# Layer 2's blocks without layer 3's steps among the scores, more steps per network tile, tokens turned one tile earlier, and pins behind the gelus

## The chip, the cores and the metric

The kernel runs on one core of a Trainium2 chip. Five engines work side by side, each through its own queue in order: TensorE (PE; its weight loads are shown apart as PEld), VectorE (DVE), ScalarE (ACT), GpSimd (POOL) and SyncE (SP), which here issues most DMAs. The metric is the device time of one execution in microseconds. The median of 8 runs before the change is 2606.69 us (2600.69 to 2609.49).

## What is computed

A tower of four layers over 8 sequences of 256 tokens with 512 channels, all in float32. Each layer adds a gated attention to the context and then a gated network. The part that matters is layer 2 and the attention of layer 3:

```python
def _L2_xattn_ref(q, k, v):
    scaled = jnp.einsum('bsd,bse->bde', q, k) * scale
    attn = jax.nn.softmax(scaled, axis=1)
    return jnp.einsum('bde,bse->bsd', attn, v)
...
def _L2_ffn_ref(x, proj1, proj1_bias, proj2, proj2_bias, gate_w):
    h = jax.nn.gelu(jnp.einsum('lne,he->lnh', x, proj1) + proj1_bias, approximate=False)
    return jnp.einsum('lnh,eh->lne', h, proj2) + proj2_bias
...
            def step(carry, kv_t):
                aa, bb, pp = carry
                ww = u + kt
                q = jnp.maximum(pp, ww)
                y_t = (exp(pp - q) * aa + exp(ww - q) * vt) / (exp(pp - q) * bb + exp(ww - q))
                q2 = jnp.maximum(pp + w, kt)
                new_carry = (exp(pp + w - q2) * aa + exp(kt - q2) * vt, exp(pp + w - q2) * bb + exp(kt - q2), q2)
...
    x = x + jnp.tanh(g_xattn[2]) * _L2_xattn_ref(_layernorm(x, axis=-1), ctx_2048, ctx_2048)
    x = x + jnp.tanh(g_ffn[2]) * _L2_ffn_ref(_layernorm(x, axis=-1), ...)
    x = x + jnp.tanh(g_xattn[3]) * _L3_xattn_ref(8, 256, 512, td, tf, _layernorm(x, axis=-1), ctx_2048)
    x = x + jnp.tanh(g_ffn[3]) * _L3_ffn_ref(_layernorm(x, axis=-1), ...)
```

Layer 2's attention is channel by channel (a 512x512 matrix for each sequence). Layer 3's attention is a recurrence along the tokens; its network is a mixture of 8 experts with 2 shared ones, for which each token's two experts are chosen ("routing").

## The kernel before

The tokens are 16 tiles of 128 (`xt[t]`), in 4 blocks of 4 tiles (512 tokens, two sequences). `back()` computes layers 2 and 3. Its order is: attention of block 0 and 1 (`xattn2`), network of block 0 (`ffn2`), attention 2, network 1, attention 3, network 2, network 3, then layer 3's shared experts (`shared3`) and routed experts.

`xattn2` makes, for each of its two sequences (`bb`), four score tiles `s`. For each, VectorE takes the maximum (L1562, L1563), ScalarE the exponential `E` with its sum (L1564), and VectorE divides the context by the sum (L1567, L1568, tile `kxvs`). Then four products `o`, two for each sequence, are added to `xt` by VectorE (L227, `add_scaled`).

`ffn2` goes through the 2048 hidden units in four groups `q` of 512. Four tiles `h2p` of hidden units (gelu on ScalarE, L1628) are followed by four output tiles `o2f` (added by L227). One weight load `p` of 512 KB on SyncE belongs to each hidden tile; 7 are held.

Between these, other work is spread in small steps. A generator in `rest` is advanced by `step(n, behind)`, n steps at a time, wherever a score, a hidden tile or an output tile has been issued; its first VectorE instruction of each step (`held`) is ordered behind the instruction given as `behind`. For the network of block 0 the generator is `later_results`: it loads and adds the last sums of layer 1's experts (`combine`: three loads `more` on SyncE and three additions L1529 for each token tile) and loads two blocks of context. Afterwards it is `tail(blk)`: layer 3's attention for a block whose layer 2 is done (`xattn3`), followed by its routing (`route`). `xattn3` normalises and turns the tokens, then for each of four groups of 128 channels runs scans `pp`, the terms `q` and `ex`, one exponential of 2048 elements a partition (L1685), the scans `aa` and `bb`, and the quotient (`num`, `den`, a reciprocal of 3.35 us, L1711). At the end the result is turned back (L1723). At the first output tile of a network's last group `last` runs what is left of the generator (`step(1000)`). In `shared3` the steps go on with the tail of block 3, until 18 pieces of it are issued; then the table of the choices is completed and read back (`slots`, `who_ps`), which the routed experts wait for.

`ready2` is a second generator, for the network of the block before: it normalises that block's tokens among the second sequence's scores (four advances) and turns them (`tr_f`, two tiles at an advance) among the products (two advances).

Instructions are put into their queues at build time, by a scheduler that goes by the order of the program and by when their inputs are ready. `behind(one, other, ...)` sets an order for that scheduler alone and adds no semaphore. The exponential and the gelu need different tables on ScalarE, so a change from one to the other is preceded by a table load.

Of the kernel before, what the change touches and what calls it, by code (L numbers as in the profile page):

```python
# [14 lines left out]
AF = mybir.ActivationFunctionType  # L15
# [7 lines left out]
KC = C // P  # L23
# [26 lines left out]
def flamingo_kernel(ctx: ExitStack, tc: tile.TileContext, a):  # L50
    nc = tc.nc
# [82 lines left out]
    def behind(one, other, reason):  # L134

        tc.add_manual_dep(
            one.ins,
            other.ins.name,
            mybir.DependencyInfo(mybir.DependencyClass.NoSync, mybir.DependencyReason.SCHED_ONLY),
            reason=reason,  # L140
        )
# [71 lines left out]
    def matmul_k(ps, lhsT, rhs):  # L213
        n = len(lhsT)
        for k in range(n):
            one = nc.tensor.matmul(ps, lhsT[k], rhs[k], start=(k == 0), stop=(k == n - 1))  # L216
            if k == 0:
                first = one
        latest[:] = [one]
        return first  # L220

    def mmtile(name):
        return mm.tile([P, BLK], F32, tag="mm", name=name)

    def add_scaled(i, ps, scale):

        return nc.vector.scalar_tensor_tensor(xt[i], ps, scale, xt[i], ALU.mult, ALU.add)  # L227
# [1285 lines left out]
                pass  # L1513


    def combine(tiles, after=(), adds=None, pool=None):

        for t in tiles:
            for u in range(SUMS1):
                if pool is not None and u < 2:  # L1520
                    if u == 0:
                        both = pool.tile([P, 2, C], F32, tag="b8", name=f"more{t}")
                    more = both[:, u, :]
                else:
                    more = t2.tile([P, C], F32, tag="t2", name=f"more{t}_{u}")
                one = nc.sync.dma_start(more, results[u][ts(t, P), :])
                for other in after:
                    behind(one, other, "not before it in the queue")
                add = nc.vector.tensor_tensor(xt[t], xt[t], more, ALU.add)  # L1529
                if adds:  # L1530
                    behind(add, adds[0], "its place")
                    adds[:] = [add]
        return one
# [3 lines left out]
    def load_kx(b, b8, after=None):  # L1537
        t = b8.tile([P, 4 * C], F32, tag="b8", name=f"kxvs{b}")
        kx = t[:, 0 : 2 * C].rearrange("p (t e) -> p t e", t=2)
        one = nc.sync.dma_start(kx, a["ctx"][ts(b, S), :].rearrange("(t p) e -> p t e", p=P))  # L1540
        if after is not None:
            behind(one, after, "not before it in the queue")
        kx_load[:] = [one]
        return kx, t[:, 2 * C :].rearrange("p (k s) -> p k s", k=KC)

    def xattn2(blk, xns, pools, step, ready=iter(())):


        scale = 1.0 / float(np.sqrt(C))
        parts = []  # L1550
        for bb in range(BLK // S):
            b = blk * (BLK // S) + bb
            kx, vs = kxvs.pop(b) if b in kxvs else load_kx(b, pools[0])
            E = pools[bb].tile([P, KC, C], F32, tag="b8", name=f"E{b}")
            parts.append((vs, E))
            z = sm.tile([P, KC], F32, tag="z2", name=f"z2_{b}")
            m = sm.tile([P, KC], F32, tag="m2", name=f"m2_{b}")
            for ec in range(KC):
                ps = mmtile(f"s2_{b}_{ec}")
                matmul_k(ps, [kx[:, t, ts(ec, P)] for t in range(2)], [xns[bb * 2 + t] for t in range(2)])  # L1560
                c1 = slice(ec, ec + 1)
                nc.vector.tensor_reduce(m[:, c1], ps, AX.X, ALU.max)  # L1562
                nc.vector.tensor_scalar(m[:, c1], m[:, c1], -scale, None, ALU.mult)  # L1563
                nc.scalar.activation(  # L1564
                    E[:, ec, :], ps, AF.Exp, bias=m[:, c1], scale=scale, accum_out=z[:, c1]
                )
                nc.vector.reciprocal(z[:, c1], z[:, c1])  # L1567
                one = nc.vector.tensor_scalar(  # L1568
                    vs[:, ec, :], ctxT[blk][:, ec, ts(bb, S)], z[:, c1], None, ALU.mult
                )  # L1570
                if bb:
                    latest_dve[:] = [one]
                    next(ready, None)
                else:
                    step(1, one)
        for bb, (vs, E) in enumerate(parts):
            b = blk * (BLK // S) + bb
            for nt in range(2):
                ps = mmtile(f"o2_{b}_{nt}")
                other = latest[0]  # L1580
                one = matmul_k(
                    ps, [vs[:, ec, ts(nt, P)] for ec in range(KC)], [E[:, ec, :] for ec in range(KC)]
                )
                if bb == 0 and nt == 0:
                    behind(one, other, "the last scores first")
                if bb:
                    next(ready, None)
                one = add_scaled(blk * TB + bb * 2 + nt, ps, tg[:, 2:3])
                step(1, one)


    turned2, latest_dve = {}, []

    def ready2(blk, b8, gb2):

# [16 lines left out]
    def ffn2(blk, b8, wp, b1, gb2, step, last, write):  # L1612
        xT = turned2.pop(blk)

        for q in range(HID // BLK):
            h = b8.tile([P, KC, BLK], F32, tag="b8", name=f"h2_{q}_{blk}")
            p2 = []
            for j in range(KC):
                c = q * KC + j
                w = wp.tile([P, 2 * C], F32, tag="w", name=f"p12_{blk}_{c}")  # L1620
                one = nc.sync.dma_start(w, a["p12"][c])
                if blk == 0:
                    behind(one, first_loads[0], "not before it in the queue")
                p1 = w[:, 0:C].rearrange("p (k o) -> p k o", k=KC)
                p2.append(w[:, C:])
                ps = mmtile(f"h2p_{q}_{blk}_{j}")
                matmul_k(ps, [p1[:, k, :] for k in range(KC)], [xT[:, k, :] for k in range(KC)])
                one = nc.scalar.activation(h[:, j, :], ps, AF.Gelu, bias=b1[:, c : c + 1])  # L1628
                if q == 0:
                    t = blk * TB + j  # L1630
                    nc.gpsimd.tensor_tensor(out=xt[t], in0=xt[t], in1=gb2, op=ALU.add)
                step(2 if q < 1 else 3, one)
                write(1, latest[0])
            for i in range(TB):
                ps = mmtile(f"o2f_{q}_{blk}_{i}")
                matmul_k(ps, [h[:, j, ts(i, P)] for j in range(KC)], p2)
                one = add_scaled(blk * TB + i, ps, tg[:, 6:7])
                step(1, one)
                if q == HID // BLK - 1:
                    last(i)  # L1640

# [9 lines left out]
    def xattn3(blk, b8, lp, u, w, held):  # L1651
# [4 lines left out]
        for c in range(KC):  # L1656
# [7 lines left out]
            bb = lp.tile([P, NS, S + 1], F32, tag="bb", name=f"bb{nm}")  # L1664
# [11 lines left out]
            ex = b8.tile([P, 4, NS, S], F32, tag="b8", name=f"ex{nm}")  # L1676
            q = t2.tile([P, NS, S], F32, tag="t2", name=f"q3_{nm}")
# [4 lines left out]
            held(nc.vector.scalar_tensor_tensor(ex[:, 2], p0, wc, p1, ALU.add, ALU.subtract))  # L1682
            yield
            nc.gpsimd.tensor_tensor(out=ex[:, 3], in0=k, in1=p1, op=ALU.subtract)
            nc.scalar.activation(ex, ex, AF.Exp)  # L1685
            yield
            ev = t2.tile([P, NS, S], F32, tag="t2", name=f"ev3_{nm}")
            nc.gpsimd.tensor_tensor(out=ev, in0=ex[:, 3], in1=v, op=ALU.mult)
# [30 lines left out]
        other = latest[0]  # L1719
        for i in range(TB):  # L1720
            ps = tr.tile([P, KC, P], F32, tag="tr", name=f"y3_{blk}_{i}")
            for c in (KC - 1, *range(KC - 1)):
                one = nc.tensor.transpose(ps[:, c, :], xnT[:, c, ts(i, P)], ident)  # L1723
# [8 lines left out]
    def back():  # L1732
        with ExitStack() as st:
# [110 lines left out]
            place = []  # L1844
# [8 lines left out]
                        reason="spread over the other block's products",  # L1853
                    )

            rest = []

            def step(n, behind=None):

                for _ in range(n):  # L1860
                    if rest:
                        place[:] = [behind] if behind is not None else []
                        if next(rest[0], True):
                            rest.pop()
# [19 lines left out]
            for bb in range(BLK // S):  # L1884
                tiles = (2 * bb, 2 * bb + 1)
                loaded = combine(tiles, kx_load) if bb else first_loads.pop()
                kxvs[bb] = load_kx(bb, bp, loaded)
                xns += norm_of(tiles, f"a2{bb}_")
                other = latest_norm[0]
# [6 lines left out]
            loaded = combine(range(TB, 2 * TB))  # L1896
# [50 lines left out]
            def later_results():  # L1947

                for t in range(2 * TB, TT):
                    loaded = combine((t,))  # L1950
                    yield
                for blk in range(2, NB):
                    context(blk, loaded)
# [164 lines left out]
            one, other = nc.tensor.matmul(cnt, onesb, run[:, TT, :], start=True, stop=True), latest[0]  # L2118
# [93 lines left out]
            other = latest[0]  # L2212
            for n in range(2):
                one = nc.tensor.transpose(who_ps[:, n, :], slots[:, :, n], ident)
# [229 lines left out]
```

## Time and profile before

| | |
|---|---|
| median of 8 runs | 2606.69 us |
| profiled execution, its own time | 2604.53 us |
| its span, first to last instruction | 2602.6 us |
| mean granted TensorE clock | 0.980 |
| busy in the span: PE, DVE, POOL, ACT | 2451.3, 1277.4, 902.2, 643.6 us |

The stages that the change touches, from the busy time in stretches of the span (us; the clock is the granted TensorE clock):

| stretch | what | PE busy | DVE busy | ACT busy | clock |
|---|---|---|---|---|---|
| 1474 to 1509 | attention 1 | 30.37 of 35 | 34.10 | 7.40 | 0.96 |
| 1620 to 1663 | attention 2 | 36.00 of 43 | 33.18 | 10.47 | 0.92 |
| 1662 to 1780 | network 1 | 116.16 of 118 | 81.15 | 28.86 | 1.00 |
| 1780 to 1822 | attention 3 | 34.32 of 42 | 34.23 | 10.48 | 0.96 |
| 1821 to 1943 | network 2 | 118.17 of 122 | 82.11 | 29.73 | 1.00 |
| 1943 to 2066 | network 3 | 118.33 of 123 | 88.28 | 35.28 | 1.00 |
| 2066 to 2235 | first shared experts | 164.52 of 169 | 97.97 | 36.28 | 0.98 |

In the lines of the profile, a name such as `o<-E,kxvs` says what is written from what, `x24` how many records are merged, and a float32 product of 512 columns is two records for each 128 rows. In a timeline the first number is the start and the second the length; the bracket holds the engine's idle time before the line and what ended it. In the view of the waits the numbers are the total, the count and the longest.

### The profile page before, as it was taken

How to read it: one execution, taken by the hardware profiler on the slowest of the kernel's cores; microseconds unless marked ns; L12 is line 12 of the kernel's file. 1: busy time of each engine (PE TensorE's matmuls, PEld its weight loads, DVE VectorE, ACT ScalarE, POOL GpSimd, SP SyncE). 2: the span in 40 equal slices, each digit the busy share in tenths (PEclk: the TensorE clock that was granted, in tenths of full speed). 3: DMA queues.
4: the chain of work that ended last, by engine and by line, in shares of the span. 5: the costliest groups of instructions: out<-in, count | busy, mean ns of one | idle time of the engine just before them, and what ended most of it. 6: DMA issues, size and time to landing. Idle time of an engine off the chain costs nothing. (4 is left out here: it accounts for less than half of the span.)

```text
span 2602.6 us, 29842 instructions
## 1 busy us (share of the span) xinstructions
PE 2451.3 (94%) x10389; PEld 1260.1 (48%) x10404; DVE 1277.4 (49%) x3518; ACT 643.6 (25%) x1451; POOL 902.2 (35%) x843
## 2 busy tenths in 40 slices
PE   7889898999999989999999999898999999999997
PEld 3444454446655635555554344444444444455553
DVE  6656665635656542222222932668676676111111
ACT  1544444411111112222222211222223222111110
POOL 1110201121455355566664010332424252444442
PEclk9999999989999999999999999999999999999999
DMA  5000010011312248899996822021121212898984
GB/s 222 5 21 21 21 41 5 20 52 49 83 33 66 64 144 223 237 303 252 296 241 131 280 100 101 19 101 63 65 97 65 109 17 49 268 291 291 310 292 82
DMA packets 102179, 333.75 MB, mean 128 GB/s; under 512 B 23287, under 2 KB 25720, under 8 KB 93826
## 3 DMA queue, kind: packets, MB, share of 16 engines
q0 software_dynamic: 48256, 148.74, 21.7%
q1 hardware_dynamic: 50354, 178.73, 19.8%
q10 hardware_dynamic: 3408, 4.25, 0.5%
q8 instruction: 87, 1.43, 0.2%
q14 instruction: 74, 0.61, 0.1%
HBM read 283.35 MB, written 66.88 MB: 135 GB/s over the span
## 5 line engine op out<-in xcount | busy, mean ns | idle before, releaser
L1335 PE MATMUL gu<-w,eb 128*128 128x352 f32 (+1 forms) x1064 | 241.0, 463 | 3.3 <-DMA w<-in_w 3.3
L216 PE MATMUL h2p<-xnT_f,p 128*128 128x512 f32 x512 | 226.6, 598 | 5.9 <-issue 4.5
L216 PE MATMUL o2f<-p,h 128*128 128x512 f32 x512 | 226.0, 595 | 3.3 <-ACT h L1628 3.2
L1370 POOL DMA_INDIRECT acc<-eb,who x94 | 147.4, 1568 | 132.8 <-DVE eb L105 104.1
L546 ACT ACTIVATE pr<-pr,n 128x256 f32<-128x256 f32 x256 | 127.9, 501 | 150.7 <-DVE n L541 145.8
L1335 PEld LDWEIGHTS gu<-w,eb 128*128 128x128 f32 (+1 forms) x1064 | 130.2, 160 | 72.1 <-issue 19.8
L1012 POOL DMA_INDIRECT table<-pay,rowi x128 | 125.8, 983 | 107.7 <-issue 23.5
L216 PEld LDWEIGHTS h2p<-xnT_f,p 128*128 128x128 f32 x512 | 97.1, 192 | 123.1 <-issue 119.6
L216 PEld LDWEIGHTS o2f<-p,h 128*128 128x128 f32 x512 | 95.9, 190 | 122.4 <-issue 114.5
L1387 POOL DMA_INDIRECT xg<-xnd,who x94 | 99.4, 1057 | 51.1 <-issue 17.1
L227 DVE SCALAR_TENSOR_TENSOR x<-o2f,tg,x 128x512 f32<-128x512 f32 x64 | 46.9, 741 | 124.8 <-PE o2f L216 123.4
L598 POOL TENSOR_TENSOR y<-y,gbo 128x512 f32<-128x512 f32 x16 | 20.4, 1273 | 245.7 <-DVE y L597 238.1
L169 POOL TENSOR_TENSOR rstd_a<-ve_a,mhalf 128x4 f32<-128x4 f32 x15 | 15.6, 1043 | 257.0 <-DVE ve_a L167 257.0
L1984 PE MATMUL g_r<-w3gu,xgT 128*128 128x352 f32 (+1 forms) x336 | 102.6, 468 | 0.7 <-ACT xgT L107 0.7
L541 DVE CUSTOM_DVE_ANT_0 pr<-s,mask 128x256 f32<-128x256 f32 x256 | 96.7, 416 | 11.2 <-PE s L521 6.8
L1984 PE MATMUL u_r<-w3gu,xgT 128*128 128x352 f32 (+1 forms) x336 | 100.0, 459 | 0.0
L1993 DVE SCALAR_TENSOR_TENSOR h_r<-a_r,share,u_r 128x352 f32<-128x352 f32 x33 | 19.1, 580 | 160.7 <-PE u_r L1984 157.4
L1628 ACT ACTIVATE h<-h2p,b 128x512 f32<-128x512 f32 x64 | 43.4, 686 | 213.5 <-PE h2p L216 213.3
L2010 PE MATMUL d_r<-w3d,hT_r 128*128 128x512 f32 (+3 forms) x252 | 96.1, 596 | 0.0
L553 PE MATMUL pt<-ident,pr 128*128 128x128 f32 x512 | 85.1, 285 | 9.8 <-ACT pr L546 5.8
L1406 PE MATMUL ed<-w,eb 128*128 128x512 f32 (+1 forms) x266 | 91.2, 601 | 0.9 <-DVE eb L1356 0.9
L105 DVE COPY eb<-ed 128x512 f32<-128x512 f32 x47 | 32.5, 692 | 119.3 <-PE ed L1406 119.3
(586 smaller groups left out, 4718.7 us busy)
## 6 DMA issues: line engine op xcount, KB each, us to landing
w<-in_w SPq DMA_DIRECT2D x64, 960.0 KB, 8.0
p<-in_p SPq DMA_DIRECT2D x64, 512.0 KB, 4.8
acc<-xnd SPq DMA_DIRECT2D x48, 256.0 KB, 5.8
more<-acc SPq DMA_DIRECT2D x48, 256.0 KB, 3.7
xnd<-xn_f SPq DMA_DIRECT2D x32, 256.0 KB, 4.3
wd<-in_wd SPq DMA_DIRECT2D x64, 96.0 KB, 7.8
ctxTa<-in_ctxT SPq DMA_DIRECT2D x4, 1024.0 KB, 5.0
x<-in_x SPq DMA_DIRECT2D x16, 256.0 KB, 6.1
```

The source lines that it names most:

```text
L216: one = nc.tensor.matmul(ps, lhsT[k], rhs[k], start=(k == 0), stop=(k == n - 1))
L227: return nc.vector.scalar_tensor_tensor(xt[i], ps, scale, xt[i], ALU.mult, ALU.add)
L541: one = nc.vector.tensor_tensor_reduce(pr[:, nt, :], ps[r][:, nt, :], mask[:, nt, :], -1.0, -LOW, ALU.add, ALU.min, n16[:, nt, h : h + 1],)
L546: nc.scalar.activation(pr[:, nt, :], pr[:, nt, :], AF.Exp, bias=n16[:, nt, h : h + 1], scale=-1.0, accum_out=s16[:, nt, h : h + 1],)
L553: nc.tensor.transpose(pt_ps[:, lt, nt, :], pr[:, nt, ts(lt, P)], ident)
L1012: one = nc.gpsimd.indirect_dma_start(out=table[:, :], out_offset=bass.IndirectOffsetOnAxis(ap=rows, axis=0), in_=choice, in_offset=None, b ...
L1335: one = nc.tensor.matmul(gu[part, 0 : 2 * I1], xT[:, k, part], e.gu[:, k, :], start=(k == 0), stop=(k == KC - 1))
L1370: one = nc.gpsimd.indirect_dma_start(out=acc[0][:, :], out_offset=bass.IndirectOffsetOnAxis(ap=index[:stop, col : col + 1], axis=0), in_=s ...
L1387: nc.gpsimd.indirect_dma_start(out=xg, out_offset=None, in_=xnd[:, :], in_offset=bass.IndirectOffsetOnAxis(ap=who[:, col : col + 1], axis= ...
L1406: one = nc.tensor.matmul(ps[n][part, :], t.hT[rows, k, part], wd, start=(k == 0), stop=(k == 1))
L1984: one = nc.tensor.matmul(ps[part, 0:I3], xTt[:, k, part], wgu[k][:, g, :], start=(k == 0), stop=(k == KC - 1))
L2010: one = nc.tensor.matmul(ps[part, :], hT[:cn, n, part], wd[n][:cn], start=(n == 0), stop=(n == 2))
```

## The change

Among the first sequence's scores, and at its two products, blocks 2 and 3 no longer advance the generator. The second advance of the turns moves from the last product to the first of the second sequence, and the first from there to the last of the first sequence: two turns after the second product, two after the third. In the networks, a hidden tile now always gives three steps (two in the first group before) and an output tile two (one before). In `xattn3` there is one more step in each group of channels, ahead of the exponential; while `calm` is false, that is during the steps behind the third hidden tile of a group, the exponential isn't issued and the step is spent on waiting; and it is ordered behind the last gelu issued. The late sums of `later_results` are ordered behind the gelu (or addition) that the step was given.

```diff
-    def combine(tiles, after=(), adds=None, pool=None):
+    def combine(tiles, after=(), adds=None, pool=None, place=()):
...
                 add = nc.vector.tensor_tensor(xt[t], xt[t], more, ALU.add)
+                for other in place:
+                    behind(add, other, "the turned tokens first")
...
                 if bb:
                     latest_dve[:] = [one]
                     next(ready, None)
-                else:
+                elif blk < 2:
                     step(1, one)
...
-                if bb:
+                if bb != nt:
                     next(ready, None)
                 one = add_scaled(blk * TB + bb * 2 + nt, ps, tg[:, 2:3])
-                step(1, one)
-
-
-    turned2, latest_dve = {}, []
+                if blk < 2 or bb:
+                    step(1, one)
+
+
+    turned2, latest_dve, units, calm = {}, [], [], [True]
...
                 one = nc.scalar.activation(h[:, j, :], ps, AF.Gelu, bias=b1[:, c : c + 1])
+                units[:] = [one]
+                calm[0] = j != KC - 2
...
-                step(2 if q < 1 else 3, one)
+                step(3, one)
+                calm[0] = True
...
                 one = add_scaled(blk * TB + i, ps, tg[:, 6:7])
-                step(1, one)
+                step(2, one)
...
             nc.gpsimd.tensor_tensor(out=ex[:, 3], in0=k, in1=p1, op=ALU.subtract)
-            nc.scalar.activation(ex, ex, AF.Exp)
+            yield
+            while not calm[0]:
+                yield
+            behind(nc.scalar.activation(ex, ex, AF.Exp), units[0], "the hidden units first")
...
-            rest = []
+            rest, passed = [], []
 
             def step(n, behind=None):
 
+                if behind is not None:
+                    passed[:] = [behind]
                 for _ in range(n):
...
                 for t in range(2 * TB, TT):
-                    loaded = combine((t,))
+                    loaded = combine((t,), place=passed)
                     yield
```

## The prediction

> **What bounds the kernel now.** I read the page's engine table and slices first (TensorE is busy in 2451.3 of 2602.6 us, so only its gaps and its slow stretches can be won), then TensorE's waits from 1440 to 2210 us, where layer 2 and layer 3's first half run. The page's chain of waits ends in the last store at once and tells nothing of this stage. The waits (total, times, longest):
>
> ```profile
> PE o L216 <- ACT E L1564: 11.2, 2, 5.6
> PE h2p L216 <- issue: 4.5, 2, 3.2
> PE o2f L216 <- ACT h L1628: 3.2, 3, 1.2
> PE tr_f L194 <- DVE xnT_f L105: 1.5, 1, 1.5
> ```
>
> The largest wait occurs twice, once in each of the attention blocks 2 and 3, not in 0 and 1. TensorE's timeline shows block 2 (start, length, idle time before in brackets):
>
> ```profile
> 1620.73 7.03 PE L216 MATMUL s<-xn_a,kxvs 128*128 128x512 f32 x16
> 1630.54 7.03 PE L216 MATMUL s<-xn_a,kxvs 128*128 128x512 f32 x16
> 1643.21 13.64 PE L216 MATMUL o<-E,kxvs 128*128 128x512 f32 x24 [5.64 <-ACT E L1564]
> 1662.71 14.00 PE L216 MATMUL h2p<-xnT_f,p 128*128 128x512 f32 x32 [0.68 <-ACT xnT_f L107]
> ```
>
> The scores are done at 1637.6 and the next product waits for their exponentials, then runs slowly: 24 records take 13.64 us where block 1 needs 10.46. Who is late is in VectorE's timeline:
>
> ```profile
> 1640.82 0.69 DVE L1691 TENSOR_TENSOR_SCAN aa<-ex,ev 128x256 f32<-128x256 f32 x1 [2.57 <-POOL ev L1688]
> 1641.43 0.67 DVE L1562 TENSOR_REDUCE m<-s 128x1 f32<-128x512 f32 x1
> ```
>
> The maximum of a score tile stands behind a scan of layer 3 that waits for GpSimd, which waited for layer 3's exponential. Blocks 0 and 1 run before layer 3 has steps. Block 1, the model of what is to come, has no gap in scores and products, but one at its end:
>
> ```profile
> 1474.46 13.91 PE L216 MATMUL s<-xn_a,kxvs 128*128 128x512 f32 x32
> 1488.20 10.46 PE L216 MATMUL o<-E,kxvs 128*128 128x512 f32 x24
> 1504.45 1.09 PE L194 MATMUL tr_f<-ident,xn_f 128*128 128x128 f32 x8 [1.47 <-DVE xnT_f L105]
> 1508.70 16.06 PE L216 MATMUL h2p<-xnT_f,p 128*128 128x512 f32 x32 [3.16 <-issue]
> ```
>
> VectorE again, in this order: a turned tile's copy waits behind six late sums.
>
> ```profile
> 1504.32 3.69 DVE L1529 TENSOR_TENSOR x<-x,more 128x512 f32<-128x512 f32 x6
> 1507.92 0.68 DVE L105 COPY xnT_f<-tr_f 128x512 f32<-128x512 f32 x1
> ```
>
> **The change, part by part.** A clean attention block by these rows is 13.74 (score start to product start in block 1) + 13.74 (32 product records at the same pace) + 2 x 0.88 (the turns, next start minus start) = 29.2 us.
>
> *Block 1's end* (late sums pinned, turns one tile earlier). From 1474.46 to 1508.70 are 34.2 us, plus 2.1 for the slow start of the hidden products (16.06 against 13.9 for 32): 36.4 against 29.2, gain 7.1. The 24 sums move behind the first three gelus; they are 24 x 0.65 = 15.6 us on VectorE, which does 3.0 and 1.5 us of work in the two slices of 20 us from 1520: hidden. Their loads are not pinned but share the 8 buffers of `t2`, so 16 of them wait on SyncE for sums, and each takes 1.19 us to issue there (12 in 14.29): some 19 us, in the old times from the first gelu at 1516 to 1535, then the two context loads (2.1) and, behind them, the eighth weight load, landing 5.1 after its issue: 1542. Its tile starts at 1546.5 (1508.7 + 27.5 + three tiles of 3.43). Four us to spare, if the sums keep pace with the loads: 0 to 5 us lost, and I take 1, nearer to the rows.
>
> *Blocks 2 and 3* (no layer 3 steps among the first scores and products). 41.98 and 41.49 us now, first score to first hidden product. The four turns of layer 3's tokens that stand in them are not saved but moved (4 x 0.44 = 1.8), so 31.0 each: gains 11.0 and 10.5. The clock is part of it: the weight loads after the 5.64 us gap come 0.86 us apart instead of 0.43, seven times, 3.0 us.
>
> *Earlier turns.* They now stand 20.6 us after the first score (13.74 + 2 x 3.43). VectorE must have the tokens by then: the scores of the first half pace it, the second half costs 2.2 us a tile (0.68 + 0.14 + 0.16 + 0.35 and the statistics 0.69 + 0.18), so the last is done at about 16.3, variance and root on GpSimd 1.4, first two tiles 0.96 each: 19.6. One us of margin. I take 1 us lost in each of three blocks; bounds 0 and 3.5 (in block 2 the first normalised tile came 10.2 us after the product's start, the slot is at 6.9).
>
> *Exponentials behind gelus, and one step more per channel.* The last gelu of a group came late three times, 0.89, 1.22 and 1.12 us at TensorE, each time behind an exponential with two table loads (1.28 + 1.91 + 1.28). I take 2.4 of 3.2. The pins set an order and add no semaphore. Nothing is queued in ScalarE behind the moved ones but the next gelu, whose product tile has three more PSUM banks.
>
> *More steps per tile.* A layer 3 tail has 1 + 4 x 12 + 4 + 4 + 8 = 65 steps; up to the flush 8 + 12 + 16 + 16 + 13 = 65 are offered. Now it is 69 (13 a channel), offered 2 + 3 x 20 + 14 = 76; for block 2's tail, which has no attention beside it, 57 become 74, so its routing isn't flushed at the end. Routing's stalls at block ends (0.27, 0.28, 1.10, 1.03) give 1.0 of 2.7. The 2.37 and 2.14 at 2066 us are not won: the shared weights there are issued only at 2063.93 and the first lands 4.1 later.
>
> The price is on VectorE. Twenty steps per 27.5 us give a channel 13 / 20 x 27.5 = 17.9 us. Its work is 15.1 us of instructions (fourth channel, 1723.04 to 1742.6, less waits of 3.3 and 1.2) plus 2.6 residual adds of 0.75: 17.1 if its waits are filled, 21.5 if not. Four channels late by 3.6 are 14.4 us; an output tile may be read 10.3 us late (three tiles) before its bank stops TensorE. So 0 to 4 us per block, three blocks: 0 to 12, taken as 3, as the next channel's instructions are free to fill the waits.
>
> Against this speaks the Trainium skill, "SBUF — State Buffer", section "Who interferes with whom": a VectorE instruction with two SBUF inputs and a GpSimd instruction that reads SBUF exclude each other for a whole instruction. The trace agrees in kind: `q` took 1.16 us at least, 1.57 in the median and 3.00 at most. If every GpSimd instruction of a channel (five of 1.4) blocked VectorE fully, a channel's shortest spans (11.8 together) would become 18.8 and the forecast some 4 us higher.
>
> *The last tail.* Beside the shared experts 73 steps are offered up to the flush; 71 were needed, now 75. Four steps later, layer 3's outputs are turned back after the second group of down products and not among the first (2181.6 and 2183.4 now; the group ends at 2192.7): routing and its table some 6.5 us later. The table's gather lands about 2233, used at 2234.6, and tokens already wait 1.32. Ready down products (5.5 us after that wait) cover part: 0 to 6.5 lost, taken as 3.
>
> **Sum.** 7.1 + 11.0 + 10.5 - 3 (turns) + 2.4 + 1.0 - 1 (weights) - 3 (VectorE) - 3 (table) = 22.0 us. The profiled execution is 2604.53 us (span 2602.6), 2.2 below the median of 2606.69; so 2582.5 by its own time, about 2584.7 as a median. I say 2584.
>
> **Rivals.**
> *The turns wait* (chance 0.15). If the normalised tokens keep their place relative to the products, TensorE loses 3.3 us at each of three blocks and half its clock for a few tiles more: 3 x 2.3 beyond what I took, and about 1.5 each for the clock: 2584 + 11 = 2595. For it: POOL's root and four normalisations follow the last statistics. Against: block 2's lateness came from the steps that leave.
> *The table is late* (0.10): the full 6.5 and a cold start of TensorE, with the weights 5 late: 2584 + 3.5 + 2 + 4 = 2593. For it: the wait of 1.32 is there already.
> *VectorE becomes the bound* (0.11), the slower side. From channels 2 to 3 the first scans are 24.4 us apart (1698.63 to 1723.04). At that length the lag is 4 x 6.5 = 26 us, 15.7 beyond the banks, in three blocks 47: 2584 + 44 = 2628. It decides from (10.3 + 8.3) / 4 + 17.9 = 22.5 us a channel, where 25 us are gone. Against: that distance was paced by the old steps, and VectorE is busy in 81.15 of 118 us there; 12 more from the attention are 93 of 118.
> *The steps were not the cause* (0.07): the exponentials are late by themselves, 2606. Against: block 1, with VectorE busy in 34.10 of 35 us and no steps, has no such wait.
>
> **Numbers.** The forecast has 0.57, its own range 2575 to 2592. The whole range reaches the first two rivals and the full prices of VectorE and table (25 us nearly spent): 2574 to 2604. About 0.2% (5 us) can be told from no change: faster 0.57 + 0.15 + 0.10 = 0.82, same 0.07, slower 0.11.
>
> **What would show it.** Right: no wait of `o` for `E`; 31 us from first score to first hidden product in blocks 2 and 3; no sums on VectorE before the first gelu; the clock at 1.00 through both blocks. Wrong: `h2p` or `o2f` waiting for the residual add (L227), turns waiting for `xn_f`, a longer wait of the gathered tokens or of `who_ps`, hidden products waiting for weights in the second group. I am wrong altogether if layer 3's tails still run at the next flush.

## The result, and the profile after

The changed kernel is slower. Its median is 2614.62 us in 12 runs (2611.33 to 2620.21), beside 2604.58 us for the kernel before in 33 runs; the ratio is 1.004 with a 95% interval of 1.0031 to 1.0048. The profiled execution took 2614.68 us with a span of 2612.9, against 2604.53 and 2602.6 before: 10.3 us of span more. The prediction was 2584 and faster.

Lines of TensorE's waits from 1440 to 2260 us of the kernel after (total, times, longest), to be put beside the waits of before in the prediction:

```profile
PE o2f L216 <- ACT h L1631: 17.1, 3, 6.4
...
PE tr_a L194 <- DVE xnT_f L105: 4.5, 2, 3.0
PE sg L216 <- DMA shgu<-in_shgu: 4.4, 1, 4.4
PE y L1732 <- POOL xnT_a L1722: 3.2, 2, 2.0
...
PE who_ps L2225 <- DMA slots<-table,row_t: 2.6, 1, 2.6
```

The 11.2 us of `o` for `E` and the 4.5 of `h2p` are gone, as the change meant. In their place stands a wait of 17.1 us of the output tiles `o2f` for the gelu's result `h`, which was 3.2 before.

Where in the span this happens is read from the first starts of TensorE's tiles, which cut the span into pieces without a remainder:

| from, to | before | after | difference |
|---|---|---|---|
| start to first score of block 0 | 1441.98 | 1441.55 | -0.43 |
| to first score of block 2 (attention 0 and 1, network 0) | 178.75 | 173.43 | -5.32 |
| attention 2 | 41.98 | 35.35 | -6.63 |
| network 1 | 117.69 | 124.91 | +7.22 |
| attention 3 | 41.49 | 35.24 | -6.25 |
| network 2 | 121.46 | 131.31 | +9.85 |
| network 3 | 125.28 | 133.60 | +8.32 |
| first shared product to first routed product | 177.94 | 181.65 | +3.71 |
| routed experts to the end | 356.03 | 355.86 | -0.17 |
| sum | 2602.6 | 2612.9 | +10.3 |

So 18 us were won in front and in the attention, and 25.4 lost in the three networks that have layer 3's attention beside them.

TensorE's timeline of the kernel after, attention 2 (start, length, idle time before in brackets):

```profile
1614.98 7.03 PE L216 MATMUL s<-xn_a,kxvs 128*128 128x512 f32 x16
1622.80 7.11 PE L216 MATMUL s<-xn_a,kxvs 128*128 128x512 f32 x16 [0.79 <-DMA kxvs<-in_ctx]
1629.74 7.03 PE L216 MATMUL o<-E,kxvs 128*128 128x512 f32 x16
1645.94 1.09 PE L194 MATMUL tr_a<-ident,xn_a 128*128 128x128 f32 x8 [3.02 <-DVE xnT_f L105]
1650.33 13.90 PE L216 MATMUL h2p<-xnT_f,p 128*128 128x512 f32 x32
```

Scores and products follow each other; the products run at full pace (16 in 7.03), and the granted clock is 1.00 from the first score to the first hidden product of both blocks. What is left is a turn of layer 3's tokens, `tr_a`, that waits 3.02 us for a copy on VectorE. At the end of block 1 the first hidden product starts without a wait, and the late sums come after it (timelines of TensorE and of VectorE):

```profile
1505.11 13.90 PE L216 MATMUL h2p<-xnT_f,p 128*128 128x512 f32 x32
```

```profile
1505.98 5.50 DVE L1529 TENSOR_TENSOR x<-x,more 128x512 f32<-128x512 f32 x9
```

The loss, in TensorE's timeline: the third group's outputs in network 1, and the same place in networks 2 and 3.

```profile
1691.53 13.90 PE L216 MATMUL o2f<-p,h 128*128 128x512 f32 x32
1705.26 13.90 PE L216 MATMUL h2p<-xnT_f,p 128*128 128x512 f32 x32
1718.99 1.02 PE L216 MATMUL o2f<-p,h 128*128 128x512 f32 x2
1724.47 9.08 PE L216 MATMUL o2f<-p,h 128*128 128x512 f32 x14 [4.46 <-ACT h L1631]
1734.80 0.66 PE L1732 MATMUL y<-ident,xnT_a 128*128 128x128 f32 x4 [1.25 <-POOL xnT_a L1722]
...
1886.36 8.36 PE L216 MATMUL o2f<-p,h 128*128 128x512 f32 x14 [6.19 <-ACT h L1631]
...
2020.96 11.89 PE L216 MATMUL o2f<-p,h 128*128 128x512 f32 x20 [6.42 <-ACT h L1631]
```

Two groups run without a gap. In the third the outputs stop after the first few records. And the work after the gap is slow: 14 records in 9.08 us, where 32 take 13.90, so 14 take about 6.1. ScalarE's timeline of the same stretch shows who is late, and VectorE's last line before it whom that one waited for:

```profile
1708.94 1.28 ACT L1631 ACT_TABLE_LOAD   x1 [6.66 <-PE h2p L216]
1710.23 0.69 ACT L1631 ACTIVATE h<-h2p,b 128x512 f32<-128x512 f32 x1
1719.22 1.28 ACT L1694 ACT_TABLE_LOAD   x1 [8.30 <-issue]
1720.51 1.91 ACT L1694 ACTIVATE ex<-ex 128x2048 f32<-128x2048 f32 x1
1722.44 1.28 ACT L1631 ACT_TABLE_LOAD   x1
1723.73 1.84 ACT L1631 ACTIVATE h<-h2p,b 128x512 f32<-128x512 f32 x3
```

```profile
1717.39 1.76 DVE L1688 SCALAR_TENSOR_TENSOR ex<-pp,w 128x512 f32<-128x512 f32 x1
```

This is the place to learn from. ScalarE does one gelu at 1710.23 and then stands for 8.3 us, though TensorE finishes a second and a third hidden tile meanwhile and the fourth at its end (four tiles from 1705.26 to 1719.16). The next instruction of its queue is the exponential of the fourth group of channels ("channel" from here on), and that is not ready: VectorE writes its last input until 1719.15. The view calls the releaser "issue" here, but 1719.22 follows 1719.15 at once, and at the same place in network 3 it names VectorE's `ex`:

```profile
2015.70 1.28 ACT L1694 ACT_TABLE_LOAD   x1 [9.02 <-DVE ex L1685]
```

The three gelus behind the exponential (two in network 3) are then done in one go, and 0.74 us after the start of that go TensorE goes on. ScalarE took its instructions in order here, so the exponential that stood too early in the queue held up gelus that were ready; `e1` below tests this.

The exponentials themselves are evenly spaced: in network 1 they start at 1659.39, 1679.98, 1700.37 and 1720.51, in network 2 at 1819.54, 1841.56, 1861.95 and 1882.39, so 20.1 to 22.0 us apart and mostly about 20.4. That is the pace at which VectorE (with GpSimd and ScalarE) finishes a channel.

### The profile page after: what moved, and what is told of

It reads as the page before. It is cut to its first block, busy times and chain, and to the rows that moved or that the text cites. A ratio compares the mean times of both kernels' runs of the same rounds, so it can differ in the third digit from the quotient of the medians.

```text
span 2612.9 us, 29842 instructions
## 1 busy us (share of the span) xinstructions
PE 2452.9 (94%) x10389; PEld 1260.1 (48%) x10404; DVE 1281.9 (49%) x3518; ACT 653.0 (25%) x1458; POOL 904.2 (35%) x843
## 3 DMA queue, kind: packets, MB, share of 16 engines
q1 hardware_dynamic: 50354, 178.73, 19.6%
## 5 line engine op out<-in xcount | busy, mean ns | idle before, releaser
L216 PE MATMUL o2f<-p,h 128*128 128x512 f32 x512 | 234.4, 614 | 17.2 <-ACT h L1631 17.1
L1335 PEld LDWEIGHTS gu<-w,eb 128*128 128x128 f32 (+1 forms) x1064 | 129.6, 159 | 71.3 <-issue 17.1
L598 POOL TENSOR_TENSOR y<-y,gbo 128x512 f32<-128x512 f32 x16 | 20.4, 1273 | 246.9 <-DVE y L597 239.4
L169 POOL TENSOR_TENSOR rstd_f<-ve_f,mhalf 128x2 f32<-128x2 f32 (+1 forms) x16 | 14.0, 873 | 253.1 <-DVE ve_f L167 253.1
L227 DVE SCALAR_TENSOR_TENSOR x<-o2f,tg,x 128x512 f32<-128x512 f32 x64 | 46.6, 733 | 107.8 <-PE o2f L216 107.7
L216 PE MATMUL sg<-xnT_f,shgu 128*128 128x512 f32 x192 | 88.8, 604 | 4.4 <-DMA shgu<-in_shgu 4.4
L553 PEld LDWEIGHTS pt<-ident,pr 128*128 128x128 f32 x512 | 60.1, 144 | 65.1 <-issue 28.7
```

Of the source, the lines that this page charges most:

```text
L553: nc.tensor.transpose(pt_ps[:, lt, nt, :], pr[:, nt, ts(lt, P)], ident)
L1335: one = nc.tensor.matmul(gu[part, 0 : 2 * I1], xT[:, k, part], e.gu[:, k, :], start=(k == 0), stop=(k == KC - 1))
```

## The experiments

My theory after the result (A) was the queue: the faster steps issue the fourth exponential at a place in ScalarE's queue that its input can't reach in time, and the gelus behind it pay. One rival (B) was that VectorE's chain is the bound by itself, so that moving the exponential only moves the wait; another (C) that the pins do the harm, by holding the exponentials behind gelus. Each kernel was run beside the kernel before on the same chip. The medians of before differ by up to 1.5 us between these sessions (2604.58 to 2606.11), so differences to the kernel after are good to about that much.

**The fourth exponential after its group's gelus** (`e1`). The only change to the kernel after: in the third group no exponential is issued before the fourth gelu.

```diff
-                calm[0] = j != KC - 2
+                calm[0] = j != KC - 2 and not (q == 2 and j < KC - 1)
```

> The changed kernel, but in a network's third group no exponential of layer 3 is issued before the last gelu, so the fourth channel's exponential stands behind all four gelus (69 us after the first hidden product, where VectorE has its input ready) and not behind the first (58 us). Theory A (the exponential, queued ahead of gelus and not yet ready, holds ScalarE): the three waits of o2f for h (17.1 us in all) and the slow clock after them (about 10) go, some 5 us come back as waits for the turned results: 2590 us, between 2583 and 2598. Theory B (VectorE has too much to do in the networks, and the wait on the gelu only shows it): the time comes back at other waits, 2607 to 2616.

Measured: 2589.95 us beside 2606.09, ratio 0.9942 (0.9925 to 0.9959): 24.7 us less than the kernel after, from a later place of three exponentials in one queue. (The steps spent on waiting also put off what follows the exponential in its channel, down to `y`; the waits of `y` go from 3.2 to 1.3 us, the small part of the gain.) The timelines of its TensorE and ScalarE in network 1, and from the waits over 1440 to 2240 us the line of the outputs, in this order:

```profile
1707.33 13.90 PE L216 MATMUL h2p<-xnT_f,p 128*128 128x512 f32 x32
1721.06 13.90 PE L216 MATMUL o2f<-p,h 128*128 128x512 f32 x32
```

```profile
1712.30 0.69 ACT L1631 ACTIVATE h<-h2p,b 128x512 f32<-128x512 f32 x1
1714.39 0.69 ACT L1631 ACTIVATE h<-h2p,b 128x512 f32<-128x512 f32 x1 [1.41 <-PE h2p L216]
1717.83 0.69 ACT L1631 ACTIVATE h<-h2p,b 128x512 f32<-128x512 f32 x1 [2.75 <-PE h2p L216]
1721.26 0.69 ACT L1631 ACTIVATE h<-h2p,b 128x512 f32<-128x512 f32 x1 [2.75 <-PE h2p L216]
1721.96 1.28 ACT L1694 ACT_TABLE_LOAD   x1
1723.26 1.91 ACT L1694 ACTIVATE ex<-ex 128x2048 f32<-128x2048 f32 x1
```

```profile
PE o2f L216 <- ACT h L1631: 1.1, 1, 1.1
```

The four gelus now wait for TensorE only, and the exponential starts 70.9 us after the network's first hidden product (1652.39), where the kernel after had it at 70.2. So it is not later by any amount that counts, although it stands four places further back: it had never been able to run earlier. The wait of `o2f` falls from 17.1 to 1.1 us and network 1 lasts 116.74 us. This rejects B: with the same work on VectorE the gap is gone.

**Without the pin on the exponential** (`e2`): the kernel after with the exponential as before, without the additional step, the waiting and the order behind a gelu.

```diff
-            yield
-            while not calm[0]:
-                yield
-            behind(nc.scalar.activation(ex, ex, AF.Exp), units[0], "the hidden units first")
+            nc.scalar.activation(ex, ex, AF.Exp)
```

> The changed kernel without the added step, the calm flag and the order behind the gelu: the exponentials go where the scheduler at build time thinks them ready. The third then stands before the last gelu of the second group and the fourth before the first gelu of the third group, both further ahead of VectorE's pace of some 20.4 us a channel than in the changed kernel. Theory A: two waits of o2f for h in each network, 8 and 5 us before the clock; 2622 to 2645 us. Theory C (pinning the exponentials is what delays the gelus): 2600 or less. Theory B: no more than 5 us from the changed kernel.

Measured: 2633.14 us, ratio 1.0107 (1.0086 to 1.0127), 18.5 us worse than the kernel after. Its waits, 1440 to 2260 us:

```profile
PE o2f L216 <- ACT h L1631: 25.7, 3, 10.8
PE y L1729 <- POOL xnT_a L1719: 13.2, 3, 4.9
```

This rejects C, which wanted 2600 or less. That the pin itself softens the harm isn't shown: the pin, the waiting and the added step went together, and without the step a channel is offered sooner. I had looked for two waits on gelus in each network; there was one, up to 10.8 us long, and beside it another of the same kind in TensorE's own queue: `y`, the turning back of layer 3's results, stands among the products at a place where GpSimd hasn't finished them, and the products behind it wait.

**The old pace** (`e3`): the kernel after with the step counts of before.

```diff
-                step(3, one)
+                step(2 if q < 1 else 3, one)
...
-                step(2, one)
+                step(1, one)
```

> The changed kernel with the old number of steps (two or three a hidden tile, one an output tile). The exponentials come behind the second gelu of group 0 and 1, the first of group 2 and the last of group 2, each after VectorE has its input. Theory A: no wait of o2f for h above 1.5 us, 27 us gained on the changed kernel, of which a flush of about ten steps at each network's end gives back 0 to 5 us each: 2588 to 2603. Theory C: 2610 or more, since the pin is still there.

Measured: 2596.13 us, ratio 0.9961 (0.9943 to 0.9979). No wait of `o2f` for `h` is left in its list, but others are longer than in the kernel before, where they are 1.6 us and nothing (1440 to 2260 us):

```profile
PE tr_f L194 <- DVE xn_f L179: 6.5, 2, 5.1
PE y L1732 <- POOL xnT_a L1722: 4.3, 1, 4.3
```

**The new pace alone** (`e6`): the kernel before with three steps for every hidden tile and two for an output tile (the reverse of the last diff, on the kernel before).

> The kernel before with nothing but more steps per tile (three a hidden tile, two an output tile). Theory A: little is lost in networks 1 and 2, where the first channel is begun in the attention (0 to 3 us each), but in network 3 the third and fourth exponential stand before the last gelu of the second and the first gelu of the third group, 14 us or more ahead of VectorE, so that o2f waits for h two times there: 2628 us, between 2615 and 2640. If the number of steps were harmless without the pins: 2600 to 2608.

Measured: 2647.08 us, ratio 1.0158 (1.0142 to 1.0173). The sign is as expected, but the time lies 19 us above the expected one and outside its range. Its waits, 1440 to 2260 us:

```profile
PE y L1723 <- POOL xnT_a L1713: 23.6, 3, 9.4
PE o2f L216 <- ACT h L1628: 12.1, 2, 10.8
PE o L216 <- ACT E L1564: 11.4, 2, 5.7
```

I had priced the gelus and not `y`, which costs more. In network 3 one wait on a gelu came (10.8) and not two. Together the first two lines are 35.7 us, against 3.2 in the kernel before; its span (2644.9) is 42.3 longer.

Before, after and these three are put in order by one number, the distance at which the program offers a channel's exponentials: the steps of a channel, over the steps given in a group of 27.5 us (from the second group on). It is worked out from the code; what VectorE keeps is the measured 20.4. `e2` and `e6` offer the exponentials sooner still, and within a network they start 19.6 to 23.4 us apart there all the same.

| kernel | steps a channel | steps a group | offered distance | median |
|---|---|---|---|---|
| before | 12 | 16 | 20.6 us | 2604.58 |
| pace alone (e6) | 12 | 20 | 16.5 us | 2647.08 |
| after | 13 | 20 | 17.9 us | 2614.62 |
| after, no pin (e2) | 12 | 20 | 16.5 us | 2633.14 |
| after, old pace (e3) | 13 | 16 | 22.3 us | 2596.13 |

The upper two lack the gains in the attention, the lower three have them. In each group the time is lower with the offer slower than 20.4 us and higher with the offer quicker; between 17.9 and 20.6 no kernel was run. At 17.9 the fourth channel is ahead by four times 2.5, which is 10 us: its place in the queue, behind the first hidden tile of the third group, comes about 58 us after the first hidden product (2 x 27.5 + 3.4), and its input came at 69. The number doesn't decide alone: `e1` offers at 17.9 too and doesn't pay, as no gelu of the group stands behind its fourth exponential.

**The parts that gain, alone** (`e4`, `e7`). First the attention's steps, on the kernel before:

```diff
-                else:
+                elif blk < 2:
                     step(1, one)
...
-                step(1, one)
+                if blk < 2 or bb:
+                    step(1, one)
```

> The kernel before with nothing but the attention part: no layer 3 steps among the first sequence's scores and products of blocks 2 and 3. Theory A: the attention blocks take 31 us as in the changed kernel, 21 us gained, no late gelu as the old pace is kept, 0 to 5 us given back at each network's end by the flush of six steps: 2583 to 2598. Theory B (the work taken out of the attention has no room in the networks): 2600 to 2606.

Measured: 2592.12 us, ratio 0.9953 (0.9936 to 0.997). Attention 2 lasts 34.41 us and attention 3 35.32, not the 31 expected, and `o` waits for no `E`.

Then the earlier turns and the pinned sums, on the kernel before:

```diff
-                if bb:
+                if bb != nt:
                     next(ready, None)
...
+                for other in place:
+                    behind(add, other, "the turned tokens first")
```

> The kernel before with nothing but the earlier turns and the late sums behind the gelus. The wait and the slow start at the first network go (7 us) and the tile copies no longer stand behind sums: 2598 us, between 2594 and 2602. If the loads of the sums or of the weights come late instead: 2603 or more.

Measured: 2596.97 us, ratio 0.9959 (0.9945 to 0.9973). The wait of `o` for `E` is still 11.2 us here and that of `o2f` 3.3, so the two parts don't touch each other's waits. In sum they are some 23 us of gain, near what the whole was predicted to bring; but no run has just these two together. `e3`, which has both with the pin and the added step at the old pace, gains 10.0 us, so they can't be taken to add up; which wait eats the rest wasn't taken apart.

**The last tail shorter by its four steps** (`e5`): the kernel after with the additional step left out for block 3, whose tail runs beside the shared experts.

```diff
-            yield
+            if blk < NB - 1:
+                yield
```

> The changed kernel without the added step a channel in the last block's tail (beside the shared experts). Theory: those four steps make the table of choices late, so from the first shared product to the first routed product it takes some 178 us as before, not 181.7, and the waits of who_ps and of the gathered tokens (5.6 us) shrink to about 1.5: 2611 us, between 2608 and 2614. Rival: the table is late for another reason, and nothing changes (2613 to 2617).

Measured: 2609.13 us, ratio 1.0012 (1.0003 to 1.0021), 5.5 us under the kernel after. From the first shared to the first routed product it takes 177.87 us, as before (177.94), and the wait of `who_ps` is gone from its list; the gathered tokens still wait 2.4 us, where 1.5 were expected. The wait of `o2f` for `h` is as it was (17.0 us), so the two losses are separate.

**All of it mended** (`e8`): the late fourth exponential, the short last tail, and no step at all in attention 2 and 3 (`if blk < 2:` in place of `if blk < 2 or bb:`).

> The kernel with the late fourth exponential, the short last tail, and no layer 3 steps at all in the attention of blocks 2 and 3, so that the turns of layer 3's tokens (waits of 5.8 us in all for xnT_f and xn_a) move into the networks. Theory A: 2590 less 3 (table) less 5 (turns): 2582 us, between 2576 and 2588. If the first channel then starts so late that the exponentials are late again: 2590 or more.

Measured: 2581.84 us beside 2606.11, ratio 0.9909 (0.9895 to 0.9923), faster than both. Its attention 2:

```profile
1613.05 7.03 PE L216 MATMUL s<-xn_a,kxvs 128*128 128x512 f32 x16
1621.03 7.10 PE L216 MATMUL s<-xn_a,kxvs 128*128 128x512 f32 x16 [0.95 <-DMA kxvs<-in_ctx]
1627.97 7.03 PE L216 MATMUL o<-E,kxvs 128*128 128x512 f32 x16
1644.22 3.67 PE L216 MATMUL h2p<-xnT_f,p 128*128 128x512 f32 x8 [0.50 <-issue]
1647.73 1.04 PE L194 MATMUL tr_a<-ident,xn_a 128*128 128x128 f32 x8
```

Attention 2 takes 31.17 us and attention 3 30.37. The turns `tr_a`, four of about 0.44 us in each, now stand among the hidden products and wait for nothing; so part of the gain only moved, and network 1 takes 120.13 us (116.74 in `e1`). The two together are 151.30 us against 154.33. The expected 2582 was met with wrong terms: in the profiled executions, `e8` is 2.0 us shorter than `e1` from the first score of block 2 to the first shared product, where 5 were expected of the turns, and 6.6 from there to the first routed product (174.23 and 180.83), where 3 were expected of the table; 1.9 more lie ahead of block 0's first score.

## Why the prediction was wrong

**The step that failed** is the price of more steps per tile: "an output tile may be read 10.3 us late (three tiles) before its bank stops TensorE. So 0 to 4 us per block, three blocks: 0 to 12, taken as 3", together with "Nothing is queued in ScalarE behind the moved ones but the next gelu, whose product tile has three more PSUM banks". The lag was seen: 17.9 us offered, 17.1 to 21.5 needed, and the measured 20.4 lies between, nearer to the end where VectorE's waits aren't filled. But I followed the lag along VectorE, to the residual additions and their banks, and there nothing was lost: no product waits for an addition (L227) in the list. The lag cost where another engine's queue had the late instruction built into it. And "the next gelu" was three gelus (two in network 3), since further hidden tiles are finished while the exponential waits. A free bank helps TensorE to write a hidden tile; the output tile needs the gelu done. The networks lost 25.4 us, where the prediction had them gain 0.4 (2.4 and 1.0 less 3). That is 25.8 of the 32.3 us between the forecast gain of 22.0 and the span's loss of 10.3; 6.6 more are the attention blocks below. The estimate of 18.8 us a channel with VectorE held off by GpSimd wasn't tested by itself: the measured 20.4 contains all causes, and a channel has six such GpSimd instructions of 1.3 to 1.7 us (fourth channel of network 1 before), not five.

**Blocked gelus that would gain 2.4** were wrong for the same reason: 3.2 us of waits became 17.1. `e1` shows that with the fourth exponential behind its gelus they fall to 1.1, so the step's idea holds and its place was wrong for one channel of four.

**Block 1's end** was right: 34.2 us plus a slow start became 29.39 (first score 1475.72 to first hidden product 1505.11), against 29.2 as worked out. The sums begin with the hidden products, 0.87 us after them and not behind the first gelu as I said; no TensorE wait shows it. From this block's first score to that of block 2 it takes 139.26 us, where it took 146.27: 7.0 gained, and the 1 each taken for the turns and the weights wasn't lost. The table above shows 5.3, because attention 0, from its first score to block 1's, took 34.17 us instead of 32.48: the second sequence's scores there wait 4.7 us for an exponential instead of 1.7, the scores before them ran at half the clock in before and not in after, and the slow clock comes after the gap instead. The change isn't shown to cause this, for `e2` and `e5`, with the instructions of the kernel after in that block, take 32.48 too. The 16 loads of the sums took 10.59 us to issue, 0.66 each and not 1.19, at the pace of the sums that freed their buffers (SyncE waited for a sum before each). The 1.19 was no price of issuing: in the kernel before, those 12 loads had waited some 10 of their 14.29 us for VectorE.

**Blocks 2 and 3** were right in mechanism and too large in size: 35.35 and 35.24 us instead of 31.0 each, a gain of 12.9 instead of 21.5 less 2 for the turns. The step kept at the second sequence's products turns layer 3's tokens there. In block 2 the wait of 3.02 us for VectorE's copy and 0.79 for the context's load make most of the 4.35; in block 3 the turns wait 1.45 for a copy and 1.34 for a normalised tile, and the scores 0.75 for the load, of 4.24. `e8`, without these steps, has the 31 us.

**The table** was right in mechanism and nearly in size: 3 us taken, 3.71 measured. Counted from the first shared product, the table's first write starts after 144.50 us instead of 140.97, so 3.5 late and not 6.5, and the gathered `slots` are waited for 2.6 us. At the first shared product nothing was won, as said: the 2.37 and 2.14 us of waits for routing became one of 4.4 for the shared weights.

**The rivals.** "VectorE becomes the bound" had the sign, with a wrong mechanism and a wrong point: it decided from 22.5 us a channel, where 20.4 was enough to lose, because the first to wait isn't an output bank but the gelu behind the exponential. VectorE was busy in 86.94 of the 125 us from 1650 to 1775. "The steps were not the cause" is rejected by `e4`; "the turns wait" appears in part, for layer 3's tokens rather than layer 2's. None of the signs I gave for being wrong pointed at this wait: the additions (L227) held up nothing, and the longer waits that did come, of `who_ps` and of the gathered tokens (3.0 us instead of 1.3), belong to the table. I left out the case that mattered: for each instruction that the change moves forward in an in-order queue, what happens when its input is not ready at its new place.

## What to carry to other kernels

Where work is spread through a program in steps, compare the distance at which the steps offer an instruction with the distance at which its inputs really come; if the offer is quicker, the instruction can block the queue it stands in, and it was that queue's next instructions, on another engine than the busy one, that showed the loss here. Put a late side job behind the main work of its stage rather than ahead of it: here that cost the side job under one us and gave the kernel back 24.7. A large gain in one stage is no proof of a change; cut the span at fixed tiles and ask of every stage what it paid.

## What the runs showed of the hardware

Each of the three long gaps on TensorE cost more than its length. TensorE's weight loads after the gap of 4.46 us in network 1 of the kernel after:

```profile
1724.47 0.50 PEld L216 LDWEIGHTS o2f<-p,h 128*128 128x128 f32 x2 [5.28 <-ACT h L1631]
...
1728.05 0.34 PEld L216 LDWEIGHTS o2f<-p,h 128*128 128x128 f32 x1 [0.52 <-issue]
1728.90 0.34 PEld L216 LDWEIGHTS o2f<-p,h 128*128 128x128 f32 x1 [0.52 <-issue]
...
1731.24 0.19 PEld L216 LDWEIGHTS o2f<-p,h 128*128 128x128 f32 x1 [0.24 <-issue]
1731.67 0.19 PEld L216 LDWEIGHTS o2f<-p,h 128*128 128x128 f32 x1 [0.24 <-issue]
```

They come 0.85 us apart, and from 1730.39 on 0.43 apart; the granted clock is 0.50 from 1724 to 1728 us. So the slow stretch lasts 5.9 us here; it is 4.3 us after the gap of 6.19 and 6.1 after that of 6.42. A gap of about 3 us went both ways: the turn `tr_a` waits 3.02 us in the kernel after and its eight loads take 0.86, while in `e1` it waits 3.03 and the same eight take 1.57.

The Trainium skill, "TensorE: Matmul & The Clock Gate", section "What's actually happening", states half the clock after at least one idle window of about 3.4 us, the full one after at least one busy window of that length, and that the windows run on freely. The three gaps of 4.46 to 6.42 us agree with the first. The slow stretches of 4.3 to 6.1 us are longer than one window and shorter than two, for which the second leaves room; the measured ones are what to count with. At half the pace half of a stretch is lost, here some 2 to 3 us on top of each of the three gaps.
